# A sandwich of attention and experts on one Trainium2 core: a block's closing made of two planned works, buffers for both, and GpSimd's planned work in written order

## The chip, the cores and the metric

The kernel runs on one NeuronCore of one Trainium2 chip. The metric is device time in microseconds (us) of one execution, as the median of several. A profile of one further execution gives, for each engine, what ran when and what it waited for. The engines are PE (TensorE, matmuls), PEld (its weight loads), DVE (VectorE), ACT (ScalarE), POOL (GpSimd) and SP (SyncE, which here only issues DMAs). Each engine works off its own instructions in their order, and waits on semaphores for what other engines have to deliver. "L520" is line 520 of the kernel before.

## The reference, cut to what matters

```python
# x: (4, 1024, 256), 16 heads of 16, 8 experts with 684 hidden units, 2 experts for each token
q, k, v = (layernorm(x) @ W.T + b for W, b in ...)      # q and k then get rotary positions
attn = softmax(q k.T / 4)                                # per batch and head, 1024 x 1024
x = x + layernorm(attn v @ Wo.T + bo)                    # first half of the sandwich
xs = layernorm(x)
dist = sqrt(max(|xs|^2 + |centroid|^2 - 2 xs @ centroid.T, 1e-12))
w, sel = top_k(dist, 2); w = softmax(w)
out = sum over the two selected experts of  w * (silu(xs Wg + bg) * (xs W1 + b1)) W2 + b2
x = x + layernorm(out)                                   # second half
```

## The kernel before, in words

**Stages.** First comes attention for four batches b, which the profile shows up to about 1,147 us. A tail up to about 1,240 us ends the last blocks. Then the experts' loop runs over 39 tiles of 256 tokens (L1168 on), and the results are added and stored.

**How attention is tiled.** Tokens come in 8 blocks of 512 (`TB`), two for each batch: block `b*2+h`, h being 0 or 1. Heads come in four groups g of four. A unit is one (batch, group, query half), 32 in all, in the hand-written `order` (L917). A unit has 8 steps, one for each 128 keys, so there are 256 steps, 64 for each of the first three batches. One step (`step`, L638) makes the scores on PE (`sc`, L654 and L661), their exponentials on ACT (`e`, L665), and the weighted sum of an earlier step on PE (`av`, L722). Beside it run the row maxima of later units: PE makes `pm` (L579), DVE reduces it (`part`, L583), and when a unit's maxima are all there, DVE rounds them (`mx`, L559 and L560) and PE turns them (`pmx`, L564) for the unit's first scores.

**What feeds a batch.** `prepare` (L387) loads a block of x (`xa`, L79, issued from POOL's queue), normalizes it (a Newton inverse root on POOL, L265 to L287), transposes it (`pt`) and projects it (`pp`, L445, copied by ACT to `turned`, L450). `split` (L503) is POOL's work for one group and half: `rotated` (five instructions that make `rot`, L472 to L487) and `split_up` (eight that make `split`, L495 to L498: four for the q side, four for the k side). `stack` (L511) then has PE transpose the splits (`ps`, L520) for the maxima and scores. The `split` tiles have two buffers, taken in turn.

**What closes a block.** `finish` (L730), one work of some twenty portions, does for a block: load x (`xb`, L79, one buffer), transpose the attention output (`po`, L745) into `oT`, project it (`py`, L759), add the bias into `y` (L763, DVE), its layernorm (Newton chain `t_y`, `y_y`, `off_y` on POOL), add it to x (`xb`, L775, POOL), store the sum to `resid` (SP), then a second layernorm (`t_m` chain on POOL), `xr` (L791, ACT), its transposes (`ptm`, L797) and distances to the centroids (`pdist`, L818), the choice of two experts on DVE (L824 to L853), the count of places in `both` and `run` (L860 to L865, POOL), PE's `rank` (L878), more DVE, and eight indirect DMAs that send the rows to the experts' lists (`rows`, L906, POOL). Its tiles `y`, `oT`, `nT` (tag `oT`) and `xb` have one buffer each.

**What sets the order.** Everything but the steps is a `Work` (L333): a generator that names the cost of its next portion ("P1820 D700" is 1,820 ns of PE and 700 of DVE) and then issues it. `run_one` takes the first work, by due step, whose next portion `fits` (L344). A work may start only when the works in its `after` have been issued; it isn't asked whether their results are there. `maxima` forces a group's stacks, and `step` its shift, when they are needed. In attention `tc.manual_schedule(engines={ET.PE, ET.DVE, ET.Activation})` (L969) keeps PE, DVE and ACT in the order in which the planner issued. POOL and SP are not in the set: the framework's own scheduler places their instructions, mixing works and putting loads ahead where it holds them free.

The due steps of `finish` are written by hand (L626): in the next batch, at step `(b+1)*64+16` for block 2b and `(b+1)*64+36` for block 2b+1. `prepare` of the next batch is due 22 and 16 steps before its group's maxima.

Of the kernel before, what the change touches and what calls it, by code (L numbers as in the profile page):

```python
# [19 lines left out]
NG = 4  # L20
# [23 lines left out]
def sandwich(  # L44
# [32 lines left out]
    def load_x(blk, use, q=nc.sync):  # L77
        xb = ap2.tile([P, NTB, C], F32, tag=f"x{use}", name=f"x{use}_{blk}", bufs=1)
        q.dma_start(out=xb, in_=token_rows(x_rows, blk))  # L79
        return xb  # L80
# [8 lines left out]
    misc_sb = load(const, [P, NE * NE], misc[:, 2 * P : 2 * P + NE * NE], "misc", nc.gpsimd)  # L89
    rope_sb = ap1.tile([32, T], F32, tag="y", name="rope_sb")  # L90
    nc.sync.dma_start(out=rope_sb, in_=rope[0:32, :])
# [99 lines left out]
    def late_constants():  # L191

        yield "D200"
        nc.vector.tensor_tensor(csq, cen_sb, cen_sb, ALU.mult)
        yield "P300 A250"
        pc = bank("pc")
        for k in range(KC):
            nc.tensor.matmul(pc[:, :NE], ones, csq[:, k, :], start=(k == 0), stop=(k == KC - 1))
        nc.scalar.copy(cn, pc[:, :NE])


        yield "D500"
        bvs = ap1.tile([P, KC, P], F32, tag="y", name="bvs")
        for k in range(KC):
            nc.vector.tensor_scalar(bvs[:, k, :], ones, bv_sb[:, k : k + 1], None, ALU.mult)
        yield "P500 D400"
        pc = bank("pbo")
        for k in range(KC):
            nc.tensor.matmul(
                pc[:, :C], bvs[:, k, :], wo_sb[:, k, :], start=(k == 0), stop=(k == KC - 1)  # L210
            )
        nc.vector.tensor_tensor(bo_sb, pc[:, :C], bo_sb, ALU.add)
# [40 lines left out]
    nc.gpsimd.memset(seen, 0.0)  # L253

    def inverse_root(v, shape, name, e):

# [18 lines left out]
    def norm_scales(stats, n, name, e=None):  # L275


        e = e or nc.gpsimd
        mv = small.tile([P, n, 2], F32, tag=f"mv{name[0]}", name=f"mv_{name}")
# [107 lines left out]
    def prepare(b, h, x_given=None, fast=False):  # L387

        yield "G1000 W4000"
        xb = x_given or load_x(b * NQB + h, "a", nc.gpsimd)  # L390
        stats = stats_tile(f"a{b}_{h}")
# [111 lines left out]
    def split(b, g, half, fast=False):  # L503

        e = nc.vector if fast and half else nc.gpsimd
        yield "G5500"
# [84 lines left out]
    def outputs(u, av):  # L591
# [7 lines left out]
        def turn_back():  # L599
            yield "P500 D750"  # L600
            if g == 0:
                old = divmod(b * NQB + qb - 3, NQB)
                if old in closing and old not in read:
                    closing[old].finish()
# [18 lines left out]
        back.ready = av_free[0]  # L623
        if g == NG - 1:
            closing[b, qb] = Work(
                finish(b, qb, fast=u == len(order) - 1), (b + 1) * NG * ITS + (36 if qb else 16),  # L626
                after=[back] + [closing[k] for k in closing],
            )
# [81 lines left out]
    UNIT = 4 * NTB  # L710
    shifts, closing, read = {}, {}, set()
    av_free, weighted_ready, drawn = [0], [0], [0]
# [17 lines left out]
    def finish(b, h, fast=False):  # L730


        blk = b * NQB + h
        ve = nc.vector if fast else nc.gpsimd
        yield "G1000"
        xb = load_x(blk, "b", nc.gpsimd)
        for t2 in range(NTB // 2):
            yield "P540 A550"
            if t2 == 0:
                ot = outs[b, h].rearrange("p t n d -> p t (n d)")  # L740
                oT = ap1.tile([P, KC, TB], F32, tag="oT", name=f"oT_{blk}")
            pt = bank(f"po_{blk}_{t2}", pssc).rearrange("p (k t) -> p k t", k=KC)
            for i in range(2):
                for k in range(KC):
                    nc.tensor.transpose(  # L745
                        pt[:, k, i * P : (i + 1) * P], ot[:, 2 * t2 + i, k * P : (k + 1) * P], ident
                    )
            nc.scalar.copy(oT[:, :, t2 * 2 * P : (t2 + 1) * 2 * P], pt)
        read.add((b, h))
        for t2 in range(NTB // 2):  # L750
            yield "P1820 D700"
            if t2 == 0:
                y = ap1.tile([P, NTB, C], F32, tag="y", name=f"y_{blk}")
                stats = stats_tile(f"y{blk}")
            po = bank(f"py_{blk}_{t2}").rearrange("p (t c) -> p t c", c=C)
            for i in range(2):
                t = 2 * t2 + i
                for k in range(KC):
                    nc.tensor.matmul(  # L759
                        po[:, i, :], oT[:, k, t * P : (t + 1) * P], wo_sb[:, k, :],  # L760
                        start=(k == 0), stop=(k == KC - 1),
                    )
# [3 lines left out]
            yield "D660"  # L766
            statistics(stats, y, (2 * t2, 2 * t2 + 1))
        yield "D900 G3900"
        scales = norm_scales(stats, NTB, f"y{blk}", ve)
        for t2 in range(NTB // 2):  # L770
            yield "A750 G1300"
            ts = slice(2 * t2, 2 * t2 + 2)
            for t in (2 * t2, 2 * t2 + 1):
                normalized(y[:, t, :], y[:, t, :], scales, t)
            ve.tensor_tensor(xb[:, ts], xb[:, ts], y[:, ts], ALU.add)  # L775
        yield "D660"
        nc.sync.dma_start(out=token_rows(resid, blk), in_=xb)
        stats = stats_tile(f"m{blk}")
# [6 lines left out]
        for t2 in range(NTB // 2):  # L785
            yield "A750"
            if t2 == 0:
                xr = ap1.tile([P, NTB, 2, XW], F32, tag="xr", name=f"xr_{blk}")
                nT = ap1.tile([P, KC, TB], F32, tag="oT", name=f"nTm_{blk}")
            for t in (2 * t2, 2 * t2 + 1):  # L790
# [3 lines left out]
            for i in range(2):  # L794
                t = 2 * t2 + i
                for k in range(KC):
                    nc.tensor.transpose(  # L797
                        pt[:, k, i * P : (i + 1) * P], xr[:, t, 0, k * P : (k + 1) * P], ident
                    )
            nc.scalar.copy(nT[:, :, t2 * 2 * P : (t2 + 1) * 2 * P], pt)  # L800
            for i in range(2):
# [4 lines left out]
                )  # L806
        yield "P1850 D600"
        nc.gpsimd.tensor_copy(xr[:, :, 1, :C], xr[:, :, 0, :C])
        for i in range(2):
            nc.gpsimd.tensor_scalar(  # L810
                xr[:, :, i, C + 1], token_id, float(i * B * T + blk * TB), None, ALU.add
            )


        pd = bank(f"pdist_{blk}")
        for t in range(NTB):
            for k in range(KC):
                nc.tensor.matmul(  # L818
                    pd[:, t * NE : (t + 1) * NE], nT[:, k, t * P : (t + 1) * P],
                    cen_sb[:, k, :], start=(k == 0), stop=(k == KC - 1),  # L820
                )
        sh = [P, NTB, NE]
# [3 lines left out]
        )  # L826
        nc.vector.scalar_tensor_tensor(
            d, pd[:, : NTB * NE].rearrange("p (t e) -> p t e", e=NE), -2.0, d, ALU.mult, ALU.add
        )
        nc.vector.tensor_scalar(d, d, 1e-12, None, ALU.max)  # L830
# [28 lines left out]
        both = small.tile(sh, F32, tag="both", name=f"both_{blk}")  # L859
        nc.gpsimd.tensor_tensor(both, sel[0], sel[1], ALU.add)  # L860
        run = small.tile(sh, F32, tag="run", name=f"run_{blk}")
        nc.gpsimd.tensor_copy(run[:, 0, :], seen)
        for t in range(1, NTB):
            nc.gpsimd.tensor_tensor(run[:, t, :], run[:, t - 1, :], both[:, t - 1, :], ALU.add)
        nc.gpsimd.tensor_tensor(seen, run[:, NTB - 1, :], both[:, NTB - 1, :], ALU.add)  # L865
        ve.tensor_tensor(s2, s2, v, ALU.mult)
# [405 lines left out]
```

## Time and profile before

| | |
|---|---|
| median of 3 runs (lowest to highest) | 1929.71 us (1926.88 to 1931.09) |
| the profiled execution | 1930.2 us, of which the span of its instructions is 1928.4 us |
| TensorE clock granted, mean | 0.944 of full |
| PE idle ahead of a `ps` transpose, released by POOL's `split` | 34.3 us in 4 waits |
| PE idle ahead of `pmx`, released by DVE's `mx` | 26.4 us in 11 waits |
| last `av` of attention starts | 1144.94 us |
| first matmul of the experts (`pu`) starts | 1227.93 us |

The page has a row for each engine's busy time, then the span in 40 slices of 48.2 us (the digit 9 is 90% or more busy). A wait is listed as "engine and what it was about to do <- engine and what released it: us in total, times, longest". A timeline row gives the start, the time that the merged instructions took, engine, line, operation and tiles, and in brackets the idle time ahead of it. The 64 steps of the second batch take 280.3 us by the trace (its first `bring` matmuls, L661, start at 350.4 us, the third batch's at 630.6 us), 4.4 us a step.

### The profile page before, as it was taken

How to read it: one execution, taken by the hardware profiler on the slowest of the kernel's cores; microseconds unless marked ns; L12 is line 12 of the kernel's file. 1: busy time of each engine (PE TensorE's matmuls, PEld its weight loads, DVE VectorE, ACT ScalarE, POOL GpSimd, SP SyncE). 2: the span in 40 equal slices, each digit the busy share in tenths (PEclk: the TensorE clock that was granted, in tenths of full speed). 3: DMA queues.
4: the chain of work that ended last, by engine and by line, in shares of the span. 5: the costliest groups of instructions: out<-in, count | busy, mean ns of one | idle time of the engine just before them, and what ended most of it. 6: DMA issues, size and time to landing. Idle time of an engine off the chain costs nothing.

```text
span 1928.4 us, 27447 instructions
## 1 busy us (share of the span) xinstructions
PE 1688.6 (88%) x9640; PEld 1062.4 (55%) x9640; DVE 1085.8 (56%) x2506; ACT 879.0 (46%) x1766; POOL 565.7 (29%) x1068
## 2 busy tenths in 40 slices
PE   4789899999799999799999893499999999999950
PEld 3444444444344444344444442388888888888840
DVE  6676687778487768577688735033333333333346
ACT  2367676767576767476767671011111111111103
POOL 5643433334553342652222222111111111111104
PEclk8899999999899999899999995799999999999985
DMA  8997300010000010000000000754444444444434
GB/s 255 320 293 220 115 1 1 23 34 12 23 23 1 23 34 23 1 23 12 12 23 23 23 23 33 232 192 165 165 165 165 164 165 165 165 165 165 164 123 153
DMA packets 101036, 196.99 MB, mean 102 GB/s; under 512 B 8093, under 2 KB 80436, under 8 KB 95906
## 3 DMA queue, kind: packets, MB, share of 16 engines
q1 hardware_dynamic: 83410, 160.65, 25.2%
q0 software_dynamic: 9040, 26.21, 4.1%
q10 hardware_dynamic: 8448, 8.39, 1.4%
q8 instruction: 76, 1.25, 0.3%
q14 instruction: 62, 0.51, 0.1%
HBM read 132.22 MB, written 79.86 MB: 110 GB/s over the span
## 4 chain that ended last, share of the span: by engine, by line
PE 79%; DVE 11%; POOL 3%; DMA 2%; issue 2%; ACT 2%; POOLq 0%; ACTq 0%; DVEq 0%; SPq 0%
PE pu L1091 20%; PE av L722 11%; PE pe L1110 10%; PE pm L579 10%; PE sc L654 7%; DVE part L583 6%; PE sc L661 6%; PE ps L520 3%; PE pp L445 3%; PE py L759 2%; PE pv L458 2%; PE pd L610 1%; DMA x<-resid 1%; PE pdist L818 1%; DVE mx L559 1%
## 5 line engine op out<-in xcount | busy, mean ns | idle before, releaser
L583 DVE TENSOR_REDUCE part<-pm 128x1 f32<-128x512 f32 x1024 | 646.7, 684 | 221.5 <-PE pm L579 217.7
L665 ACT ACTIVATE e<-sc 128x512 f32<-128x512 f32 x1024 | 538.2, 602 | 224.3 <-PE sc L661 217.1
L1091 PE MATMUL pu<-xT,w 128*114 128x256 f32 x1872 | 420.0, 381 | 8.2 <-DMA w<-wall 7.3
L1091 PEld LDWEIGHTS pu<-xT,w 128*114 128x114 f32 x1872 | 332.4, 179 | 77.3 <-issue 8.1
L1096 ACT ACTIVATE sil<-pu,w 114x256 f32<-114x256 f32 x234 | 110.2, 473 | 502.5 <-PE pu L1091 490.6
L1099 DVE SCALAR_TENSOR_TENSOR h<-pu,w,sil 114x256 f32<-114x256 f32 x234 | 112.8, 484 | 335.8 <-ACT sil L1096 335.8
L579 PE MATMUL pm<-stack,stack 64*128 64x512 f32 x960 | 275.4, 469 | 23.0 <-DVE part L583 20.2
L722 PE MATMUL av<-e,v 128*32 128x512 f32 x2048 | 277.5, 614 | 0.0
L1123 POOL DMA_INDIRECT res<-yo,ids x78 | 74.8, 959 | 566.1 <-DVE yo L1122 561.0
L654 PE MATMUL sc<-stack,stack 64*128 64x512 f32 x960 | 240.0, 436 | 0.1
L661 PE MATMUL sc<-shift,bring 64*128 64x512 f32 x1024 | 236.5, 403 | 3.6 <-ACT shift L568 3.5
L579 PEld LDWEIGHTS pm<-stack,stack 64*128 64x128 f32 x960 | 121.0, 186 | 212.8 <-DVE part L583 135.6
L1110 PE MATMUL pe<-w,h 114*128 114x256 f32 x936 | 214.9, 379 | 0.0
L1110 PEld LDWEIGHTS pe<-w,h 114*128 114x128 f32 x936 | 178.0, 190 | 25.2
L654 PEld LDWEIGHTS sc<-stack,stack 64*128 64x128 f32 x960 | 116.8, 187 | 63.2 <-issue 24.9
L661 PEld LDWEIGHTS sc<-shift,bring 64*128 64x128 f32 x1024 | 126.3, 187 | 27.2 <-ACT shift L568 14.6
L520 PE MATMUL ps<-ident_r,split 128*128 128x128 f32 x512 | 70.2, 267 | 35.3 <-POOL split L498 34.3
L527 ACT CAST stack<-ps 128x512 fp32r<-128x512 f32 x124 | 73.0, 594 | 60.4 <-PE ps L520 60.2
L1122 DVE TENSOR_SCALAR yo<-pe,xt 128x256 f32<-128x256 f32 x78 | 37.7, 484 | 104.0 <-PE pe L1110 104.0
L520 PEld LDWEIGHTS ps<-ident_r,split 128*128 128x128 f32 x512 | 52.9, 145 | 78.7 <-POOL split L498 36.0
L906 POOL DMA_INDIRECT rows<-xr,to x64 | 62.9, 983 | 83.2 <-DVE to L901 66.1
L722 PEld LDWEIGHTS av<-e,v 128*32 128x32 f32 x2048 | 40.9, 108 | 70.0 <-issue 65.1
(246 smaller groups left out, 1454.4 us busy)
## 6 DMA issues: line engine op xcount, KB each, us to landing
w<-wall SPq DMA_DIRECT2D x39, 1368.0 KB, 6.8
rows<-empty SPq DMA_DIRECT2D x34, 1032.0 KB, 14.3
w<-wall SPq DMA_DIRECT2D x39, 689.3 KB
wall<-in_w_dram SPq DMA_DIRECT2D x16, 684.0 KB, 5.9
xt<-rows SPq DMA_DIRECT2D x39, 258.0 KB, 3.4
wall<-in_wg_dram SPq DMA_DIRECT2D x8, 684.0 KB
xb<-in_x_dram POOLq DMA_DIRECT2D x8, 512.0 KB, 4.5
resid<-xb SPq DMA_DIRECT2D x8, 512.0 KB, 3.2
```

Of the source, the lines that this page charges most:

```text
L520: nc.tensor.transpose(ps[:, t * P : (t + 1) * P], splits[b, g, half][:, t, is_k, 2 * pr : 2 * pr + 2].rearrange("p h n d -> p (h n d)"), i ...
L579: nc.tensor.matmul(pm, q[r, t * P : (t + 1) * P], k_[r, half * TB : (half + 1) * TB], start=True, stop=True,)
L583: nc.vector.tensor_reduce(part[:, i, 2 * pr + s, half : half + 1], pm, AX.X, ALU.max)
L654: nc.tensor.matmul(sc, k_[r, kb * P : (kb + 1) * P], q[r, qb * TB : (qb + 1) * TB], start=True, stop=False,)
L661: nc.tensor.matmul(scs[s], bring[pr][r, :], shift[u][r, :], start=False, stop=True)
L665: nc.scalar.activation(e, scs[s], AF.Exp, scale=1.0 / HD**0.5)
L722: nc.tensor.matmul(av[32 * j : 32 * j + 32, :], v_aug[kb][:, 4 * g + j, :], es[j], start=(kb == 0), stop=(kb == NT - 1),)
L1091: nc.tensor.matmul(pu[:FP, i, :], w[:, c0 : c0 + FP], xT[:, k, :], start=(k == 0), stop=(k == KC - 1),)
L1096: nc.scalar.activation(sil, pu[:FP, 0, :], AF.Silu, bias=w[:FP, OG + f : OG + f + 1])
L1099: nc.vector.scalar_tensor_tensor(h[:FP, f, :], pu[:FP, 1, :], w[:FP, OG + NF + f : OG + NF + f + 1], sil, ALU.add, ALU.mult,)
L1110: nc.tensor.matmul(po[:, :C], h[:n, f, i * P : (i + 1) * P], w[:n, O2 + f * C : O2 + (f + 1) * C], start=(f == 0), stop=(f == NF - 1),)
L1123: sent = nc.gpsimd.indirect_dma_start(out=res[:, :], out_offset=bass.IndirectOffsetOnAxis(ap=ids, axis=0), in_=y, in_offset=None,)
```

## The change

`finish` is cut after the store to `resid`; the rest is a second work, `settle`. `finish` now falls due 6 steps after its unit's last step and `settle` 8 steps after, and each waits for fewer works of earlier blocks: `finish` for the earlier `finish` works and for all `settle` works but the latest, `settle` for its own `finish` and the earlier `settle` works. `y` is written into the block's own `outs` tile, which has three buffers, so the tile `y` is gone; `xb` has two buffers; `oT` and `nTm` are tiles of their own, each half a block, with one buffer. The distances come by halves too, copied to a small `dot` tile by DVE. POOL's instructions in the works go through a wrapper that keeps them in the order in which they are issued. The works for the last block (`fast`) still have their small chains on DVE.

```diff
-        xb = ap2.tile([P, NTB, C], F32, tag=f"x{use}", name=f"x{use}_{blk}", bufs=1)
+        xb = ap2.tile([P, NTB, C], F32, tag=f"x{use}", name=f"x{use}_{blk}", bufs=2 if use == "b" else 1)
...
+    class InOrder:
...
+        def __getattr__(self, op):
+            return lambda *a, **k: tc.keep_in_program_order(getattr(self.engine, op)(*a, **k))
+
+    pool = InOrder(nc.gpsimd)
...
-        e = e or nc.gpsimd
+        e = e or pool
...
-        xb = x_given or load_x(b * NQB + h, "a", nc.gpsimd)
+        xb = x_given or load_x(b * NQB + h, "a", pool)
...
-        e = nc.vector if fast and half else nc.gpsimd
+        e = nc.vector if fast and half else pool
...
-                if old in closing and old not in read:
+                if old in closing:
                     closing[old].finish()
...
+            before_ = list(settling.values())
             closing[b, qb] = Work(
-                finish(b, qb, fast=u == len(order) - 1), (b + 1) * NG * ITS + (36 if qb else 16),
-                after=[back] + [closing[k] for k in closing],
+                finish(b, qb, fast), at_step[0] + 6,
+                after=[back] + [closing[k] for k in closing] + before_[:-1],
             )
+            settling[b, qb] = Work(
+                settle(b, qb, fast), at_step[0] + 8, after=[closing[b, qb]] + before_
+            )
...
-        ve = nc.vector if fast else nc.gpsimd
+        ve = nc.vector if fast else pool
         yield "G1000"
-        xb = load_x(blk, "b", nc.gpsimd)
+        xb = load_x(blk, "b", pool)
+        y = outs[b, h].rearrange("p t n d -> p t (n d)")
+        stats = stats_tile(f"y{blk}")
         for t2 in range(NTB // 2):
+            ts = (2 * t2, 2 * t2 + 1)
             yield "P540 A550"
+            oT = ap1.tile([P, KC, 2 * P], F32, tag="oT", name=f"oT_{blk}_{t2}")
...
+        nc.sync.dma_start(out=token_rows(resid, blk), in_=xb)
+        summed[b, h] = xb
+
+    def settle(b, h, fast=False):
+
+        blk = b * NQB + h
+        ve = nc.vector if fast else pool
         yield "D660"
-        nc.sync.dma_start(out=token_rows(resid, blk), in_=xb)
+        xb = summed[b, h]
...
+            nT = ap1.tile([P, KC, 2 * P], F32, tag="nTm", name=f"nTm_{blk}_{t2}")
+            nc.scalar.copy(nT, pt)
...
+            yield "P950 D150"
...
+            nc.vector.tensor_copy(
+                dot[:, 2 * t2 : 2 * t2 + 2], pd[:, : 2 * NE].rearrange("p (t e) -> p t e", e=NE)
+            )
...
-        nc.gpsimd.tensor_tensor(both, sel[0], sel[1], ALU.add)
+        pool.tensor_tensor(both, sel[0], sel[1], ALU.add)
```

The eight indirect DMAs of a block stay outside the wrapper, and so do POOL's instructions ahead of the first step that build constants.

## The prediction

> **What bounds the kernel now.** The page comes first: PE has the largest share, and the row PEclk shows where its clock was cut.
>
> ```profile
> PE 1688.6 (88%) x9640; PEld 1062.4 (55%) x9640; DVE 1085.8 (56%) x2506; ACT 879.0 (46%) x1766; POOL 565.7 (29%) x1068
> PEclk8899999999899999899999995799999999999985
> ```
>
> The chain that ended last gives PE 79% and POOL 3%. So POOL matters only where PE waits for it. The list of waits, kept to PE, names these places:
>
> ```profile
> PE ps L520 <- POOL split L498: 34.3, 4, 11.6
> PE pmx L564 <- DVE mx L560: 26.4, 11, 11.1
> ```
>
> By window, two of the four `ps` waits are of 11.6 us (505 to 517 us, 786 to 798 us); the other two (11.0 us) are the start's, 9.5 of it at 38 us. Of the `pmx` waits one is of 11.1 us (72.7 to 83.8), one of 5.4 us (to 228.4). Beside these PE idles about 1 us in eight steps. The timeline of POOL round the first 11.6 us:
>
> ```profile
> 484.39 0.85 POOL L79 DMA_DIRECT2D xb<-in_x_dram  x1
> 497.37 0.75 POOL L79 DMA_DIRECT2D xa<-in_x_dram  x1 [12.13 <-ACT xn L292]
> 505.62 2.48 POOL L472 TENSOR_TENSOR rot<-turned,bias_qk 128x512 f32<-128x512 f32 x2 [7.50 <-ACT turned L450]
> ...
> 517.00 0.40 POOL L498 CAST split<-split 128x256 fp32r<-128x256 f32 x1
> ```
>
> POOL isn't slow here but late: it had nothing else to do for 20 us, since `prepare` of the next batch came late (behind the closing, in steps 80 to 100), and then its scheduler mixed two groups' `rot` (x2), so that the urgent split took 11.8 us. PE paid twice:
>
> ```profile
> 517.45 0.75 PE L520 MATMUL ps<-ident_r,split 128*128 128x128 f32 x4 [11.64 <-POOL split L498]
> 518.12 0.79 PE L579 MATMUL pm<-stack,stack 64*128 64x512 f32 x2
> 518.85 1.93 PE L722 MATMUL av<-e,v 128*32 128x512 f32 x8
> ```
>
> Eight `av` take 1.06 us elsewhere; the windows give clock 0.50 until about 523.2. That is 5.8 us at half speed, 2.9 us lost.
>
> The `pmx` waits have another cause. DVE before the one at 83.8, then POOL:
>
> ```profile
> 74.27 9.21 DVE L559 CAST mx<-m 128x16 fp32r<-128x16 f32 x1
> ```
> ```profile
> 82.73 0.72 POOL L479 TENSOR_TENSOR sw<-rot,turn 128x256 f32<-128x256 f32 x1
> 83.53 1.30 POOL L483 TENSOR_TENSOR rot<-rot,turn 128x512 f32<-128x512 f32 x1
> ```
>
> The cast, 0.18 us elsewhere, ended at 83.48, in POOL's first gap (83.45 to 83.53) since 63.9. The one at 222.2 took 5.79 us, and POOL's first gap was 227.96 to 228.04. POOL has no gap while two chains are mixed.
>
> Last, PE in the tail, where block 7's closing stands behind the rest of block 6's:
>
> ```profile
> 1144.94 2.50 PE L722 MATMUL av<-e,v 128*32 128x512 f32 x16
> ...
> 1159.81 0.63 PE L878 MATMUL rank<-both,above 128*128 128x32 f32 x2 [3.75 <-POOL both L860]
> 1160.67 0.64 PE L881 MATMUL rank<-run,ones 128*128 128x32 f32 x2 [0.23 <-POOL run L864]
> 1161.11 1.95 PE L745 MATMUL po<-ident,outs 128*128 128x128 f32 x8
> 1166.29 6.42 PE L759 MATMUL py<-wo,oT 128*128 128x256 f32 x16 [3.23 <-ACT oT L748]
> ```
>
> **The change part by part.** Where instructions go is read from the built programs' order on each engine, with steps counted by the score matmuls.
>
> *The two holes go.* Each costs 11.64 + 2.9 = 14.5 us, two 29.1. After the change the closings start at steps 57 and 66 (then 121 and 130), ahead of `prepare`, whose half 1 ends at step 104; its stack stands two steps later, not next. PE's work from that last `pp` to the first `ps` of half 1: five pairs of `pm` (0.40 each), two steps of scores (1.15), `pd` 0.57, two groups of `av` (1.0) = 6.9 us. POOL needs ACT's copy (0.7, from 504.9 to 505.6), a `rot` alone (97.48 to 102.96: 5.5) and four instructions of `split` (0.40+0.73+0.40+0.40): 8.2 with hand-overs. So 1.3 us of waiting stays.
>
> *A new wait.* The next group's first split now goes ahead of half 1's, so the last split of that group needs the buffer of the group's first, which PE's `ps` read at step 114. POOL stands there from about step 108, with the group after queued behind it: two `rot` and two `split` more, 21 us with this one, due at step 128, 14 steps (60 us) later. Nobody else waits for that. PE itself has only one `av` group (1.0 us) between that `ps` and the next, which needs four `split` instructions (2.0): 1.0 us. Both waits come in two batches: 2 x (1.3+1.0) = 4.6. PE idled 1.04 us and less without loss of clock, so none is added.
>
> *GpSimd in order.* A chain alone stops 0.08 us between dependent instructions; in a split in written order the longest run without a stop is 0.73+0.40+0.40+0.40 = 1.9 us. DVE should get in at the first stop. Here the Trainium skill speaks against a gain: "SBUF — State Buffer", Who interferes with whom, says that DVE and GpSimd lock a shared port pair for one instruction, and that the second to issue is blocked until the first finishes. By that a cast waits for one POOL instruction in either order (1.3 us), and the order is worth nothing. The rows show 9.2 and 5.8 us, through a dozen instructions, so I take the rows. At the start: two rotations come before the first split, which ends 0.7 later; then 0.8 of waiting (half of a run) for each of the two `mx` instructions. `pmx` at about 77.1, not 83.84: 6.7. At 222 POOL is at the end of a split and begins a rotation: 1.4 and 1.3 of waiting, 3.1 gained. Bounds 0 and 8.9, 0 and 5.6.
>
> *The clock there.* PE then idles 4.4 and 2.3 us. By the skill ("TensorE: Matmul & The Clock Gate", Why this matters for your kernels) gaps up to some 3 us cost no clock. In this trace gaps of 2.11 (122.8) and 2.42 us (1094.4) were followed by 3.4 us at half. By the rule the second place would save all of its 2.4 us (4.8 at half), by the rows 2.4-1.7 = 0.7. I take 0.7 at each place. Both together: 7.4 + 3.8 = 11.2.
>
> *The tail.* From the last `av` (end 1147.44) to `py` is 18.85 us now. With block 6 settled before, what is left: ACT's copy `ou`, PE `pd`, DVE to `outs` (2.1, as now), `po` 0.8, `oT` 0.6, hand-overs 0.3: 3.8. Gain 15.05. Given back: block 6's eight `ptm` (1.3 at full clock), `pdist` (1.95, as at 488.5) and `rank` (0.6) now lie in attention's last 12 steps, where PE has 22.7 of 23 us: 3.9; ACT's share is 5.8, and it is busy 18.8 of 23, so 4.5. `oT` with one buffer puts a copy between the halves of `py`: 0.7. Net 9.85. SP's store comes a little earlier and hides; block 7's `xb` load now stands among block 6's eight indirect DMAs (10.2 us), lands (4.5 us) some 6 us ahead of its use. The rest of the chain to `pu` is unchanged.
>
> *Small.* The 16 `dot` copies (0.2) lie beside `pm` work but for the last one (0.2, made good by a `pdist` half that starts sooner). Two closings beside rotations can make DVE's small pairs wait as four did (1.23 to 1.28): half a microsecond for each of six blocks, 3.0; bounds 0 and 8.
>
> Sum: 29.1 - 4.6 + 11.2 + 9.85 - 3.0 = 42.6. The profiled execution took 1930.2 (span 1928.4), 0.5 over the median of the runs, 1929.7. 1929.7 - 42.6 = **1887**.
>
> **The rivals.**
> - *The port isn't freed.* Short stops don't let DVE in. For: the rule, and some POOL pairs still follow without a stop. Against: three long casts ended in such stops (the third 523.83). It costs 11.2: 1898. Chance 0.18.
> - *The holes move.* A stack is again issued right after its split's issue, since the plan doesn't ask for results; the waits grow to some 6 us, with clock lost. For: this weakness stays. Against: the counts above. 2 x (6+6+3) = 30 in place of 4.6: 1912. Chance 0.08.
> - *Slower: GpSimd parks.* In written order one late instruction holds up the Newton chains behind it; ACT or DVE then waits with the exponentials or reductions behind. Place: three chains for each of six blocks, above all `t_m` behind the eight indirect DMAs (10.2 us). For a lateness L about L-1 of each is PE's; above L = 3.4 the 18 places eat the 42.6; at L = 5, 72 - 42.6 = 29 slower: 1959. Against: from 240 to 1120 us ACT waited 1.3 us for POOL and DVE none, and real steps are longer than planned ones. Chance 0.04.
> - *It does nothing*: 1930, chance 0.02; the orders do differ.
>
> **How the numbers follow.** The main case has 0.68. Its own bounds: no small cost (+3), the tail without giving back (+4), both new waits hidden (+4.6), more at the port (+4) end at 1872; the port rival with the small costs at 8 and new waits doubled end at 1908. The range 1871 to 1908 leaves out the holes' rival and the last two and a little of the rest. About 0.2% is what a measurement of this kernel can tell from no change. Faster 0.93, same 0.03, slower 0.04.
>
> **What would show it.** PE's `ps` waits on `split` near 505 and 786 gone or under 2 us each, with clock 1.0 there; DVE's longest `mx` cast under 2 us; `po` of block 7 within 3 us of the last `av`. Wrong if PE waits over 3 us at steps 106 or 114, if ACT or DVE wait on POOL, or if a cast over 5 us stays.

## The result, and the profile after

The changed kernel takes 1895.44 us (median of 4 runs, 1893.42 to 1901.81) where the kernel before took 1928.83 beside it: ratio 0.9832, 95% interval 0.9805 to 0.986, 33.4 us. The forecast was 1887.0. The profiled execution is the slowest of the four: 1901.8 us, span 1900.0; against before's profile (1930.2, span 1928.4) it gained 28.4. A second profile of the same kernel (below) has a span of 1894.2.

The page's rows for PE and its clock. The two eights of slices 11 and 17, where the holes were, are gone. PE's busy time is 11 us higher with the same 9640 matmuls: the row counts a matmul at half clock (granted share 0.5) as longer work, so it is no measure of work done. By the trace 64.8 us of PE's busy time were at half clock before and 83.4 are now; half of the difference is 9.3 of the 11.

```profile
PE 1699.6 (89%) x9640; PEld 1068.7 (56%) x9640; DVE 1067.6 (56%) x2522; ACT 880.6 (46%) x1766; POOL 572.7 (30%) x1068
...
PEclk8899999999999999999999995799999999999975
```

The list of PE's waits. The two of 11.6 us on `split` are gone (the 9.1 is the start's, which the change leaves alone); the wait on `mx` has fallen from 11.1 to 2.4 at most. The last line is new: PE waits for `pmx`, and the last thing DVE did before is `sel`, an instruction of the closing.

```profile
PE ps L531 <- POOL split L262: 15.9, 5, 9.1
...
PE pmx L575 <- DVE mx L571: 10.5, 9, 2.4
...
PE pmx L575 <- DVE sel L873: 3.8, 2, 1.9
```

POOL's timeline at the place of the old hole, and PE's. All POOL instructions of the works now have the wrapper's line, L262. POOL waits for ACT's copy here too (15.47 us; 7.50 before, behind a load), but PE isn't there yet. The rotation runs alone, 521.44 to 526.93, and its split follows at once: 1.65 us of waiting are left.

```profile
521.44 1.28 POOL L262 TENSOR_TENSOR rot<-turned,bias_qk 128x512 f32<-128x512 f32 x1 [15.47 <-ACT turned L461]
...
525.66 1.27 POOL L262 TENSOR_TENSOR rot<-rot,sw 128x512 f32<-128x512 f32 x1
527.00 0.40 POOL L262 CAST split<-rot 128x256 fp32r<-128x256 f32 x1
```
```profile
528.93 0.54 PE L531 MATMUL ps<-ident_r,split 128*128 128x128 f32 x4 [1.65 <-POOL split L262]
```

DVE's cast at the start, which took 9.21 us before:

```profile
76.35 0.18 DVE L570 CAST mx<-m 128x16 fp32r<-128x16 f32 x1
```

PE in the tail. `py` comes 3.4 us after the last `av` has ended (1132.45), where it was 18.85 us: no work of block 6 stands between.

```profile
1129.95 2.50 PE L740 MATMUL av<-e,v 128*32 128x512 f32 x16
...
1135.82 3.47 PE L771 MATMUL py<-wo,oT 128*128 128x256 f32 x8 [0.67 <-ACT oT L766]
```

By stage (stages begin at their first `bring` matmuls; us against the profile of before):

| stage | before | forecast | profile after | second profile |
|---|---|---|---|---|
| start to the first scores | 85.2 | -7.4 | -6.8 | -9.0 |
| batch 0 | 265.1 | -3.3 | -5.0 | -5.1 |
| batch 1 | 280.2 | -11.2 | -7.6 | -7.9 |
| batch 2 | 280.3 | -11.2 | -6.3 | -7.6 |
| batch 3, to the end of the last `av` | 236.5 | +5.0 | +10.7 | +8.7 |
| from there to the first `pu` | 80.5 | -14.4 | -16.1 | -15.9 |
| experts and store | 700.5 | 0 | +2.7 | +2.5 |
| sum | 1928.4 | -42.5 | -28.4 | -34.2 |

(The forecast's column is the sum of the prediction laid out by place, with its 3.0 of small costs spread by blocks closed.) Start, batch 0 and tail together gave what was forecast or a little more; the rows of batches 1 to 3 gave 14 and 11 us less together. That is the question of the experiments, beside the one whether order, place, and cut with buffers each did what the prediction says.

### The profile page after: what moved, and what is told of

Read it like the earlier page. It is cut to its first block, busy times and chain, and to the rows that moved or that the text cites. A ratio compares the mean times of both kernels' runs of the same rounds, so it can differ in the third digit from the quotient of the medians.

```text
span 1900.0 us, 27442 instructions
## 1 busy us (share of the span) xinstructions
PE 1699.6 (89%) x9640; PEld 1068.7 (56%) x9640; DVE 1067.6 (56%) x2522; ACT 880.6 (46%) x1766; POOL 572.7 (30%) x1068
## 5 line engine op out<-in xcount | busy, mean ns | idle before, releaser
L590 PE MATMUL pm<-stack,stack 64*128 64x512 f32 x960 | 267.9, 472 | 20.3 <-DVE part L594 15.5
L740 PE MATMUL av<-e,v 128*32 128x512 f32 x2048 | 281.7, 622 | 0.0
L1146 POOL DMA_INDIRECT res<-yo,ids x78 | 74.8, 959 | 567.8 <-DVE yo L1145 562.7
L671 PEld LDWEIGHTS sc<-stack,stack 64*128 64x128 f32 x960 | 114.9, 187 | 64.1 <-issue 23.2
L678 PEld LDWEIGHTS sc<-shift,bring 64*128 64x128 f32 x1024 | 120.6, 190 | 25.8 <-ACT shift L579 14.2
L531 PE MATMUL ps<-ident_r,split 128*128 128x128 f32 x512 | 69.4, 264 | 16.0 <-POOL split L262 15.9
```

The costliest lines, as they stand in the source:

```text
L531: nc.tensor.transpose(ps[:, t * P : (t + 1) * P], splits[b, g, half][:, t, is_k, 2 * pr : 2 * pr + 2].rearrange("p h n d -> p (h n d)"), i ...
L590: nc.tensor.matmul(pm, q[r, t * P : (t + 1) * P], k_[r, half * TB : (half + 1) * TB], start=True, stop=True,)
L671: nc.tensor.matmul(sc, k_[r, kb * P : (kb + 1) * P], q[r, qb * TB : (qb + 1) * TB], start=True, stop=False,)
L678: nc.tensor.matmul(scs[s], bring[pr][r, :], shift[u][r, :], start=False, stop=True)
L740: nc.tensor.matmul(av[32 * j : 32 * j + 32, :], v_aug[kb][:, 4 * g + j, :], es[j], start=(kb == 0), stop=(kb == NT - 1),)
L1146: sent = nc.gpsimd.indirect_dma_start(out=res[:, :], out_offset=bass.IndirectOffsetOnAxis(ap=ids, axis=0), in_=y, in_offset=None,)
```

## The experiments

All ratios are against the kernel before, run beside it on the same chip. It took 1925 to 1927 us there, but for three runs on one chip where it took 1940 (named below); so ratios are compared, not times.

**Order alone.** The kernel before with the wrapper on POOL's works and nothing else.

```diff
-        e = nc.vector if fast and half else nc.gpsimd
+        e = nc.vector if fast and half else pool
... (the wrapper, and the same at every other place where POOL's works issue)
```

> The kernel before with only GpSimd's planned work put in written order; the closing stays one work at its old place. Theory 1 (the order frees the port, and does nothing else for the holes): the long mx casts at 74 and 222 us fall under 2 us and pmx of the start comes 6.7 us sooner, 11.2 us gained in all; the two 11.6-us holes stay, and grow by about 1.5 us each, since in written order a whole second rotation (5.5 us) stands between the urgent rotation and its split (505.6 + 5.5 + 5.5 + 2.0 = 518.6 in place of 517.0). Sum: 8 us faster, about 1921. Theory 2 (the port is not the cause, the long casts went for another reason): casts of over 5 us stay and the time is that of before or 3 us more, 1929 to 1932. Theory 3 (the order alone closes the holes): ps waits under 4 us, about 1895.

1921.0 us, ratio 0.9962 (0.9949 to 0.9975). The long casts are gone (0.55 us at the start, 0.37 near 212 us); the start is 10.1 us shorter and batch 0 5.6. The holes stay and are a little longer. POOL and PE there:

```profile
495.61 1.26 POOL L262 TENSOR_TENSOR rot<-rot,sw 128x512 f32<-128x512 f32 x1
496.83 1.26 POOL L262 TENSOR_TENSOR rot<-turned,bias_qk 128x512 f32<-128x512 f32 x1
...
502.19 0.40 POOL L262 CAST split<-rot 128x256 fp32r<-128x256 f32 x1
```
```profile
504.14 0.75 PE L531 MATMUL ps<-ident_r,split 128*128 128x128 f32 x4 [12.49 <-POOL split L262]
```

The urgent rotation is done at 496.87; the plan has another group's rotation next, and the split follows that one. Theory 1 stands in its sum: the start is freed, and written order keeps a bad plan's order as faithfully as a good one's. (Whether batch 0's gain is the order's comes up in the next run.)

**The change without the order.**

```diff
-    pool = InOrder(nc.gpsimd)
+    pool = nc.gpsimd
```

> The changed kernel without the written order: GpSimd's instructions are again placed by the framework's scheduler. Theory 1: the closing's new place and its buffers give the tail (16 us) and most of the holes; but the scheduler again mixes two rotations at step 104 to 109, so that the urgent split takes some 5 us longer: two ps waits of 5 to 7 us with clock lost behind them (about 12 us more than the changed kernel), and the long casts are back (another 11 us). Sum: 1895 + 23 = about 1918. Theory 2 (the order is worth nothing): 1895 to 1900, casts short. Theory 3 (the gain was the order's): 1925 or more.

1916.0 us, ratio 0.9941 (0.9919 to 0.9963), against 0.9802 for the whole change on the same chip: the order is worth 26 us here, 23 were expected. DVE's cast and PE's wait:

```profile
74.52 9.23 DVE L570 CAST mx<-m 128x16 fp32r<-128x16 f32 x1
```
```profile
539.63 0.75 PE L531 MATMUL ps<-ident_r,split 128*128 128x128 f32 x4 [5.21 <-POOL split L509]
```

By stage, against the second profile of the whole change, it loses 9.3 us at the start and 8.6 and 10.9 in batches 1 and 2. So the order is worth 6 to 7 us by itself and 26 in the company of the rest. The tail is that of the whole change (63.3 us): it needs no order.

Nor does batch 0, which takes 257.1 us here (265.1 before, 260.0 in that second profile). The cast near 222 us with POOL beside it, first before and then here:

```profile
222.21 5.79 DVE L559 CAST mx<-m 128x16 fp32r<-128x16 f32 x1
```
```profile
222.06 0.73 POOL L495 CAST split<-rot 128x256 fp32r<-128x256 f32 x2
```
```profile
222.72 0.26 DVE L570 CAST mx<-m 128x16 fp32r<-128x16 f32 x1
```
```profile
222.56 0.73 POOL L506 CAST split<-rot 128x256 fp32r<-128x256 f32 x2
```

POOL runs the same instructions, mixed, and its next gap is 5.8 us away in both (228.54 here). Before, the cast stood until that gap; here it took 0.26 us. So an unbroken run of POOL can hold DVE, but needn't.

**The early place alone.** The kernel before, its closing due 6 steps after its unit.

```diff
-                finish(b, qb, fast=u == len(order) - 1), (b + 1) * NG * ITS + (36 if qb else 16),
+                finish(b, qb, fast=u == len(order) - 1), at_step[0] + 6,
```

> The kernel before with only the due step of the closing changed (6 steps after its unit's last step): one work, one buffer for y and xb, oT and nT in one tile, no written order. Theory 1 (the place of the closing does most of it): the holes are gone but for 2 to 6 us each, the tail from the last av to py is 4 to 6 us in place of 18.9, the long casts stay (9 and 6 us): about 1908. Theory 2 (the two works and the buffers are needed): the single xb and the forced order make the closing of block 2b+1 wait for that of 2b, ps or py waits of over 5 us appear or the tail keeps over 12 us: 1918 or more.

1939.5 us, ratio 1.0067 (1.0043 to 1.0091): slower than before, and 31 us off theory 1. The tail is as short as the change's (62.6), the holes are gone, but batches 1 and 2 take 292.3 and 293.3. They have three waits in the holes' place, of 4.45, 3.95 and 8.2 us, and 34 us each at half clock. The last one on POOL and DVE:

```profile
523.45 0.19 POOL L865 TENSOR_TENSOR seen<-run,both 128x8 f32<-128x8 f32 x1
...
527.24 0.20 POOL L866 TENSOR_TENSOR y_d<-y_d,v 128x8 f32<-128x8 f32 x1
```
```profile
527.47 0.20 DVE L869 RECIPROCAL over<-y_d 128x8 f32<-128x8 f32 x1 [7.71 <-POOL y_d L866]
```

DVE stands at the reciprocal for POOL's Newton chain, which the scheduler placed behind a rotation; the reductions stand behind DVE, and PE's `pm` behind them (8.19). This is the prediction's slower rival, GpSimd that parks others, here at 8.2 us of PE's time. It came with the scheduler's order, not with the written one. Neither theory had it.

**Early place and order, one work.** As the last, with the wrapper as in the first.

> The kernel before with the early due step and GpSimd in written order, but the closing still one work with one buffer for y, xb and oT/nT. Theory 1 (cutting the closing in two with buffers is needed too: as one work the second block's closing waits for the whole of the first's, starts some 14 steps later, and its last Newton chain stands on GpSimd behind a rotation and a split of the next batch, so that VectorE waits for it with the reductions behind): one wait of 4 to 8 us at pm in each of the two middle batches, start as short as with the order alone: 1915 to 1925. Theory 2 (order and place are all, the cut and the buffers do nothing but shorten the tail by little): no wait over 2.5 us between 130 us and the last av, 1890 to 1897.

1910.9 us, ratio 0.9924 (0.9908 to 0.9941). The order takes 28 us off the early place. What the cut and the buffers add on top, from 0.9924 to 0.9832 or 0.9802, is 17 to 24 us. The time is 4 us below theory 1's range, far from theory 2's, and the places aren't theory 1's: no long wait at `pm`, but 2.8 us at `pt` (prepare's chain behind eight indirect DMAs) and 3.16 at `ps`. PE there, and POOL ahead of it:

```profile
503.14 0.75 PE L531 MATMUL ps<-ident_r,split 128*128 128x128 f32 x4 [3.16 <-POOL split L262]
```
```profile
496.32 0.20 POOL L262 TENSOR_TENSOR t_d<-y_d 128x8 f32<-128x8 f32 x1 [2.04 <-DVE y_d L272]
...
501.20 0.40 POOL L262 CAST split<-rot 128x256 fp32r<-128x256 f32 x1
```

The rotation was done at 494.3. The closing's chain is written next, POOL waits 2.04 us for it and works 4.9 us on it, and the urgent split stands behind.

**Cut, buffers and order at the old due steps.** This one and two more below ran on the chip where the kernel before takes 1940.04.

```diff
-                finish(b, qb, fast), at_step[0] + 6,
+                finish(b, qb, fast), (b + 1) * NG * ITS + (36 if qb else 16),
...
-                settle(b, qb, fast), at_step[0] + 8, after=[closing[b, qb]] + before_
+                settle(b, qb, fast), (b + 1) * NG * ITS + (38 if qb else 18), after=[closing[b, qb]] + before_
```

> The changed kernel with the old due steps (the closing's in the next batch, its settling two steps behind); the cut, the buffers and the written order stay. Works start when they fit, so the due step only says who goes first: now prepare of the next batch goes ahead of the second block's settling, its last projection is one step ahead of its stack (not two), and a rotation of the next group stands on GpSimd between the urgent rotation and its split. Theory 1 (the place of the closing relative to prepare is what closes the holes): ps waits of 11 to 13 us in both middle batches as with the order alone, each batch 279 to 281 us; start and tail as in the changed kernel: 1903 to 1910. Theory 2 (the cut and the buffers close the holes, the place doesn't matter): ps waits under 4 us, 1890 to 1897.

1941.9 us, ratio 1.0015 (1.0002 to 1.0027): as slow as before, and slower than theory 1. The `ps` hole is back as theory 1 has it, 9.6 us. There is a second one that neither had, 8.0 us at `pt`. Start, batch 0 and tail keep their gains (76.0, 258.9 and 64.1 us), and batches 1 to 3 lose that again: they take 298.3, 295.7 and 246.3, the first two with 37.5 and 30.7 us at half clock. PE at the second hole, and POOL ahead of it:

```profile
429.30 1.18 PE L420 MATMUL pt<-ident,xn 128*128 128x128 f32 x4 [7.99 <-ACT xn L303]
```
```profile
418.26 0.22 POOL L262 TENSOR_TENSOR t_a<-t_a,var_a 128x4 f32<-128x4 f32 x1
418.65 1.00 POOL L929 DMA_INDIRECT rows<-xr,to  x1 [0.17 <-issue]
419.67 0.22 POOL L262 TENSOR_SCALAR t_a<-t_a 128x4 f32<-128x4 f32 x1
```

The closing's eight indirect DMAs, which are outside the wrapper, fall between the steps of prepare's Newton chain; a chain of 0.2-us steps then advances every 1.4 us. Together:

| order | early place | cut and buffers | ratio |
|---|---|---|---|
| yes | no | no | 0.9962 |
| no | yes | no | 1.0067 |
| yes | yes | no | 0.9924 |
| yes | no | yes | 1.0015 |
| no | yes | yes | 0.9941 |
| yes | yes | yes | 0.9802 and 0.9832 |

**Is it the port?** The kernel before; ScalarE makes the cast.

```diff
-            nc.vector.tensor_copy(hi, of_head)
+            nc.scalar.copy(hi, of_head)
```

> The kernel before with one line changed: the cast that rounds a unit's maxima (hi part of mx, 128x16) is made by ScalarE, not by VectorE; the subtraction behind it (lo part) stays on VectorE. GpSimd is as before, mixed and without a gap. Theory 1 (VectorE's access to SBUF is held up by GpSimd's unbroken run, whatever GpSimd's work is): ScalarE's cast takes 0.3 us or less at 74 us, so the 9.2 us go; if the subtraction (two operands) isn't held up, pmx comes at 75 to 76 us in place of 83.8 and at 223 to 224 in place of 228, some 12 us faster, 1915; if it is held up in the cast's place, it takes about 9 us and nothing is gained, 1927. Theory 2 (the long cast is a late operand, GpSimd has no part in it): ScalarE's cast or its wait is as long, pmx stays at 83 to 84 us, 1927 to 1930.

1947.0 us, ratio 1.0111 (1.0088 to 1.0134). ACT's cast takes 0.21 us, and DVE's next instruction is long in its place. DVE and POOL:

```profile
71.11 0.19 DVE L555 TENSOR_REDUCE m<-part 128x16 f32<-128x32 f32 x1
71.57 8.59 DVE L560 TENSOR_TENSOR mx<-m,mx 128x16 fp32r<-128x16 f32 x1 [0.27 <-ACT mx L559]
```
```profile
79.41 0.72 POOL L479 TENSOR_TENSOR sw<-rot,turn 128x256 f32<-128x256 f32 x1
80.21 1.27 POOL L483 TENSOR_TENSOR rot<-rot,turn 128x512 f32<-128x512 f32 x1
```

It ends at 80.16, in POOL's first gap (80.13 to 80.21) since it began. So at this place it isn't the cast, nor its operand: the subtraction stands in its place until POOL stops. But not everything DVE does is held: under the same unbroken run the reduction just before took its usual 0.19 us. The wait moved, as the second half of theory 1 has it. The further 20 us (13 in the profiled execution) were not expected; batches 1 and 2 together are 14 us longer than in before's profile. There `mx` on ACT queues with the exponentials (new `pmx` waits of 1.9 and 1.2 us in batch 1), and each has 3 to 7 us more at half clock.

**The changed kernel again.** No edit.

> The changed kernel once more, for a second profile and more times. Theory 1 (the gain that is missing against the forecast, some 8 us, is clock lost after waits of 1 to 2 us, and a wait costs clock or not by how it falls): the same waits stand at the same places within 0.3 us, but some of the 3.4-us stretches at half clock lie elsewhere or are gone, and the span follows them by half of their length; time 1893 to 1902. Theory 2 (the missing gain is added work and longer waits): the stretches at half clock lie at the same places and the span is the same within 1 us.

1890.3 us, ratio 0.9802 (0.9777 to 0.9826); span 1894.2. The waits are the same, the clock isn't. The third batch's `ps` wait in the first profile after the change, and in this one:

```profile
801.59 0.71 PE L531 MATMUL ps<-ident_r,split 128*128 128x128 f32 x4 [1.65 <-POOL split L262]
```
```profile
799.18 0.53 PE L531 MATMUL ps<-ident_r,split 128*128 128x128 f32 x4 [1.66 <-POOL split L262]
```

In the first, the clock is 0.5 for the 3.4 us from 801.7; in the second it stays 1.0. Up to the last `av` the first has 71.7 us at half clock and this one 58.0. Half of the difference, 6.8, is what the clock explains, and the last `av` ends 5.9 us earlier. So theory 1 holds for the spread between executions of one kernel, though the median is 3 us under its range. Most half-clock stretches lie at the same places in both, so they aren't chance alone.

**The maxima's work first.** Why does PE wait 1.9 us at `pmx`? The second profile's DVE and PE there:

```profile
374.80 0.69 DVE L775 TENSOR_TENSOR outs<-py,bo 128x512 f32<-128x512 f32 x1 [1.98 <-PE py L771]
375.41 2.47 DVE L594 TENSOR_REDUCE part<-pm 128x1 f32<-128x512 f32 x4
```
```profile
378.54 0.51 PE L575 MATMUL pmx<-ident_r,mx 128*128 128x128 f32 x4 [1.90 <-DVE sel L873]
```

DVE stood idle at the bias add until `py` was done; only then came the last four reductions, and `mx` behind them. The releaser that the list names, `sel`, merely came last by the profile. This happens at that add in every block: DVE's own list of waits for the first profile after the change, from 240 to 1130 us (engine, its next work, whom it waited for, us, times, longest):

```profile
DVE outs L775 <- PE py L771: 32.7, 14, 3.8
...
DVE st_m L309 <- POOL xb L262: 3.8, 3, 1.3
```

The kernel before has such waits too (25.7 us in 13), but not ahead of a unit's last maxima. The second line is all that DVE waits for POOL there. The planner took the closing first because its due step is the smaller.

```diff
-                        shifts[u] = Work(rows(), at_step[0] + 4)
+                        shifts[u] = Work(rows(), at_step[0] - 100)
```

> The changed kernel with one number changed: the work that rounds a unit's maxima and turns them (mx, pmx) goes ahead of every other planned work, so the closing's projection (py) and its bias add no longer stand between the last row maxima and mx. Theory 1 (the new pmx waits of 1.9 us come from VectorE standing at the bias add until py is done, and each costs a 3.4-us stretch at half clock): the pmx waits at about 379, 651, 926 and 1016 us go or fall under 1 us, four stretches at half clock go with at least two of them: 8 to 14 us faster than the changed kernel, 1877 to 1883. Theory 2 (those waits are free or just move on to the scores behind): within 3 us of the changed kernel, 1888 to 1893.

1876.6 us, ratio 0.9752 (0.9732 to 0.9772): the fastest kernel of this study, a little better than theory 1. The waits at 379, 651, 926 and 1016 us are gone. The first of these `pmx`, here:

```profile
371.49 0.51 PE L575 MATMUL pmx<-ident_r,mx 128*128 128x128 f32 x4
```

Only part of the gain is the bias add's. At 379 and 651 it is what holds the last reductions. At 926 two more instructions of the settling (`eq`, `gt`, 1.4 us) stand there, and at 1016 its chain from `over` to `diff` (0.8 us), with no `py` near. Waits of 1.0 us at `pm` (463 and 736 in the second profile, 466 and 738 in the first), behind the same chain and with a half-clock stretch each, are gone too. The edit moves `mx` ahead of all of these at once, so what each is worth isn't shown. The three batches in the first profile of the changed kernel, and here (start:end, length, then busy us and instructions of PE, PEld, DVE, ACT and POOL, PE's clock, DMA share and GB/s; the last row ends with the last `av`):

```profile
338.60:611.20 272.60, 260.88 (x1660) 129.75 (x1658) 198.27 (x431) 187.87 (x375) 122.16 (x256) 0.99 0.07 20
...
885.20:1132.50 247.30, 233.13 (x1516) 113.25 (x1512) 179.09 (x412) 171.56 (x350) 74.50 (x188) 0.97 0.06 21
```
```profile
334.40:601.50 267.10, 257.55 (x1660) 129.25 (x1658) 198.28 (x430) 187.14 (x375) 122.69 (x256) 1.00 0.07 21
...
871.50:1107.40 235.90, 225.61 (x1516) 111.14 (x1512) 178.71 (x412) 171.16 (x349) 73.75 (x188) 1.00 0.07 22
```

In batch 1 PE's busy time falls by 3.3 us though the matmuls are the same: half of the 6.8 us that were at half clock. Idle time falls by 2.2. In batch 3 it is 7.5 (half clock 17.1 to none: 8.5) and 3.9.

**The same in the kernel before.** The same line changed there, on the chip with 1940.

> The kernel before with the maxima's work put first, nothing else. Theory 1 (the waits at pmx of 1.9 us belong to the closing's new place, since before the closing's late due step already put it behind the maxima's work): nothing to win, 1922 to 1930. Theory 2 (putting it first helps any of these kernels by 8 to 14 us): 1912 to 1918.

1944.1 us, ratio 1.0014 (1.0001 to 1.0026): nothing to win, so the waits belong to the closing's new place (theory 1).

**A pair of buffers for oT and nTm.** On the kernel with the maxima first, same chip as the last one.

```diff
-    zero = ap1.tile([P, 4 * P], F32, tag="oT", name="zero")
+    zero = ap1.tile([P, 4 * P], F32, tag="nTm", name="zero", bufs=2)
...
-            oT = ap1.tile([P, KC, 2 * P], F32, tag="oT", name=f"oT_{blk}_{t2}")
+            oT = ap1.tile([P, KC, 2 * P], F32, tag="nTm", name=f"oT_{blk}_{t2}", bufs=2)
...
-            nT = ap1.tile([P, KC, 2 * P], F32, tag="nTm", name=f"nTm_{blk}_{t2}")
+            nT = ap1.tile([P, KC, 2 * P], F32, tag="nTm", name=f"nTm_{blk}_{t2}", bufs=2)
```

> The changed kernel with the maxima's work first (as in the run before, 1876.6 us) and, as well, one pair of buffers that oT and nTm take in turn in place of one buffer each. Theory 1 (a single buffer puts ACT's copy between the halves of py and of pdist, 0.7 us each time, on the path only in the tail): two waits of 0.7 us go in the tail, at most 2 us faster, 1874 to 1877. Theory 2 (the single buffers also hold up the closings in attention): 1870 or less.

1894.6 us, ratio 0.9767 (0.9746 to 0.9787), no difference from 0.9752 that can be told. The tail is 63.0 in place of 64.5 us, the two 0.7 us. The order of instructions is the same on every engine as without the pair, and yet this profile has waits of 1.8 to 2.1 us at 409, 681, 961 and 1040 us that the other has not; at 681 ACT began its copy of `av` 2.8 us after the last `av` matmul had ended, with no work of its own between. Whether the pair or that chip made them stays open.

**Block 6's settling out of the last batch.** First by its due step alone:

```diff
-                settle(b, qb, fast), at_step[0] + 8, after=[closing[b, qb]] + before_
+                settle(b, qb, fast), at_step[0] + (8 if b < B - 1 else 100), after=[closing[b, qb]] + before_
```

> The changed kernel with the settling of the last batch's first block put off to after attention (due 92 steps later); all else as changed. Theory 1 (the last batch grew by 10.7 us because that settling moved into it: 3.9 us of PE work and what the full engines add): the last batch falls back to about 237 us, and the tail from the last av to the first pu grows by 12 to 16 us (block 6 ahead of block 7 again): 1892 to 1897, no real difference. Theory 2 (the last batch grew by something else, clock or GpSimd's order): it stays at 245 or more while the tail grows: 1905 or more.

1891.5 us, ratio 0.9816 (0.98 to 0.9832), batch 3 245.0, tail 65.7: neither theory is tested, since a due step only ranks a work, and the planner ran it in attention all the same. Then with the earliest step that a work may have, on the kernel with the maxima first:

```diff
+                start=len(order) * NT - 1 if (b, qb) == (B - 1, 0) else 0,
```

> The changed kernel with the maxima's work first (1876.6 us in an earlier run, 0.9752 of the kernel before) and the settling of the last batch's first block held back, now by its earliest step, until the last step of attention. Theory 1 (the tail's gain is what that settling takes out of the tail, 12 to 16 us, and it costs attention no more than its own 3.9 us of PE work): the last batch falls from 236 to 232 us, the tail from the last av to the first pu grows from 64.5 to 77 to 80: 8 to 12 us slower than with it inside, 0.979 to 0.982 of the kernel before. Theory 2 (settling inside the last batch costs there as much as it saves behind): the batch falls by 8 us or more, the sum stays within 4 us, 0.974 to 0.977.

1893.2 us, ratio 0.9828 (0.9812 to 0.9843). Batch 3 falls from 236.0 to 231.3, the tail grows from 64.5 to 84.9. So settling inside costs 4.7 us and saves 20.4, more than theory 1's 12 to 16: held back, it also has its own 12.7-us wait for `rank` ahead of block 7's.

## Why the prediction was right, and where it fell short

*The holes.* Right as a mechanism: of 2 x 11.64 us of idling, 2 x 1.65 are left, and 1.3 was forecast. The experiments take apart what the prediction treated as one thing. PE's wait for the urgent split is 12.5 us with the order alone, 9.6 with order and cut at the old due steps, 5.2 with the new place and the cut but no order, 3.2 with place and order in one work, and 1.65 with all three. So both reasons in the prediction count: the stack two steps later does most, and the rotation that isn't mixed takes the 5.2 to 1.65. The clock there was 1.0 as forecast in batch 1 (528 to 535 us), but in batch 2 of the first profile it wasn't (0.66 from 801 to 806).

*The port.* Right at the start, and by luck at 222 us. At the start 7.4 us were forecast, 6.8 and 9.0 came, and leaving the order out costs 9.3 there. In all five profiles without written order a `mx` instruction takes 7.9 to 9.2 us at the start; in the nine with it none in the whole kernel takes more than 1.2. The other 3.8 us treated before's cast of 5.79 us as the fixed price of mixed work. In three other profiles with mixed work (the change without order, the early place alone, the maxima first in the kernel before) the same cast took 0.26, 0.62 and 0.27 us, and batch 0 took 257.1, 258.3 and 260.3 us. So batch 0's gain of 5 isn't shown to be the order's. One profile of the kernel before held a delay that other runs don't have. (The "third long cast", to 523.83, is `sel`, an instruction of another kind, 3.67 us.) The rule of the Trainium skill ("SBUF — State Buffer", Who interferes with whom), by which DVE stands for one GpSimd instruction, gave 0. At the start DVE stood 8.6 and 9.2 us, until the first gap of 0.08 us, so the rows were the better guide there; what decides whether DVE gets in between two POOL instructions stays open.

*The new wait at step 114.* It isn't there: 2 x 1.0 too much.

*The tail.* 15.05 less 0.7 was forecast, 16.1 and 15.9 came. The 4.5 given back was right as a term (4.7 in the last run), though its own figures give only 3.6 to 3.9 (22.7 of 23 us taken, 3.9 added). It isn't all that batch 3 lost.

*What fell short* is 9 us: 42.6 forecast, 33.4 measured. The step that failed is the small term, "half a microsecond for each of six blocks, 3.0; bounds 0 and 8", together with the sentence on the new waits, "PE idled 1.04 us and less without loss of clock, so none is added". I priced the closing's new neighbours only as port waits of DVE's small pairs. The cost is DVE's queue: the closing's instructions, above all the bias add that waits for `py`, stand ahead of the unit's last reductions and `mx`. That gives PE waits of 1.9 to 2.1 us at four unit ends and of 1.0 us at two more places, with half-clock stretches behind them. One changed number took them away: 13.7 us by the medians (1890.3 to 1876.6, on two chips), 9.6 by the ratios (0.0050 of 1927). The measured term is thus 10 to 14, not 3, of which the bias add alone is a part that no run isolates. The whole change with this put right, 0.9752, is 48 us faster than before; the forecast of 42.6 was a sum of gains about right and of one cost too small.

*The clock.* I took 2.9 us of lost clock as regained at each hole. It was, and as much came back elsewhere: batch 1 has 6.8 us at half clock after the change in place of 13.7, batch 3 17.1 in place of 6.8, and up to the last `av` both first profiles have 71.7. "PE idled 1.04 us and less without loss of clock" held in before's profile, not after. The Trainium skill ("TensorE: Matmul & The Clock Gate", Why this matters for your kernels) has gaps up to some 3 us free. Over all fourteen profiles, from 130 us to the last `av`, waits of PE of 1.8 to 3 us were followed by a stretch at half clock (beginning within 3.6 us) 42 times of 42, waits of 1.0 to 1.8 us 25 times of 48, shorter ones down to 0.6 us 3 times of 106. So the measurement decides against the rule here.

*The rivals.* That the port isn't freed, and that the holes move, are out. That GpSimd parks others is out for the change (from 240 to 1130 us 3.8 us of DVE's waits and 0.4 of ACT's), but not as a mechanism: it stands behind PE's wait of 8.2 us in the early place alone (1.0067) and of 8.0 with the old due steps (1.0015).

*Not settled.* The experts' part is 2.5 to 2.7 us longer in both profiles of the changed kernel (78.5 us at half clock in place of 72.4), and 0.5 with the maxima first (73.0). In these it goes with the clock behind the tail; but with the pair of buffers it is 2.4 longer at only 74.8. Why, no run here tells.

## What to carry to other kernels

A work that moves brings its whole queue along: look not only at what it waits for, but at what stands behind its instructions on each in-order engine, and give the work that PE needs next the better rank. Parts of such a change aren't additive: written order was worth 6 to 7 us alone and 26 with the rest, and the early place alone made the kernel slower. A long instruction seen in one profile may be that execution's: find it in other runs before it is priced as a gain. A due step only ranks; to hold a work back takes a bound that the planner obeys.

## What the hardware showed unexpectedly

- DVE's hold by GpSimd isn't a matter of the cast: a 128x16 subtraction took 8.59 us in its place (0.18 elsewhere), and ended in the first 0.08-us gap. A reduction under the same run of POOL took 0.19 us, as always.
- The hold isn't certain either: one cast near 222 us, beside the same unbroken POOL instructions, took 5.79 us in one kernel's profile and 0.26, 0.27 and 0.62 in three others.
- A PE wait of 1.65 us was followed by 3.4 us at half clock in one execution and a wait of 1.66 at the same place by none in another. One kernel's spans, 1900.0 and 1894.2 us, differ by about what that explains.
- Eight indirect DMAs of 1.0 us each on POOL, between the steps of a chain of 0.2-us instructions, slow that chain to a step every 1.4 us, and made PE wait 8.0 us.
